# Routing eight chunks as five singles and a group of three, with x added by matmul and the conditional blocks in the middle

## The chip, the core and the metric

The kernel runs on one core of one Trainium2 chip. The core has five engines with instruction streams of their own: TensorE (PE; its weight loads are shown as PEld), VectorE (DVE), ScalarE (ACT), GpSimd (POOL) and SyncE (SP, which here only issues DMAs). They meet through semaphores. Matmuls write to PSUM; everything else lies in SBUF or in DRAM. The metric is the device time of one execution in microseconds.

## What is computed

One transformer block on x of 4096 tokens by 256, in float32: adaptive layer norm, a linear attention, and a mixture of 8 experts of which each token takes 2. Cut to what matters here:

```python
h = _layernorm(x) * (1 + ca) + sa
x = x + ga * attention(h)
h = _layernorm(x) * (1 + cb) + sb
gate_probs = softmax(h @ Wg + bg)                 # 8 experts
_, top_idx = jax.lax.top_k(gate_probs, 2)
expert_mask = one_hot(top_idx, 8).sum(-2)
selected = gate_probs * expert_mask
selected = selected / (selected.sum(-1, keepdims=True) + 1e-08)
y = gelu(h @ W1[e] + b1[e]) @ W2[e] + b2[e]       # for each expert e, H = 1024
x = x + gb * sum_e(selected_e * y_e)
```

## The kernel before

**Layout.** The 4096 tokens are 8 chunks of 512 (`NCH`), each 4 tiles of 128 (`TPC`). `xs[i]` holds chunk i, `hT[i]` its normalized transpose. Attention is folded into one matrix `weff` of 256 columns (`D`) and 8 more (`E`) that give the attention's part of the gate logits; `raw` holds the part that comes from x. `hT[i] @ weff` is the residual of chunk i.

**Order.** `on.pe`, `on.dve`, `on.act`, `on.pool` and `on.sp` keep each engine's instructions in the order in which the Python code makes them, up to the end of the first five blocks. So the code's order is each engine's queue.

**Routing, per Route.** A `Norm` turns the statistics of x into `rstd` and `shift` (`variance` on DVE, `root` as Sqrt on ACT, `finish` on DVE). `distances` makes logits less their greatest, `power` is Exp on ACT, `rows` writes the normalized rows on ACT, `choose` finds the two greatest experts with ranks that break ties, `places` counts on PE, with triangular and all-ones matrices, how many earlier tokens took each expert (`both` is the mask of the two), `weigh` normalizes the weights, `aim` turns places into row numbers of the DRAM table `routed`, and `send` lets POOL scatter the rows by indirect DMA, one for each tile and choice, so 8 per chunk. `seen` carries the counts from one route to the next.

**Routes.** Chunks 0, 1 and 2 are routed singly, then a table (`early_table`) says which 256-row blocks of an expert are full already; chunks 3 and 4 are routed together, and 5, 6 and 7 together inside the first blocks. `park(i)` lets ACT take a chunk's residual out of PSUM into `hT[i]`; `add` lets DVE add it to `xs[i]` and take statistics.

**Blocks.** A block is 256 rows (a pair) or 128 rows (a single) of one expert. Its `load` issues the DMAs of w1, b1, the rows (`xg`), w2 and b2 on SP, with expert and first row read from the table `where`. `prepare` transposes the rows on PE (`ptb`) and scales them on ACT (`xT`); `hidden` is 32 matmul records `ph` with 8 Gelus `gl` on ACT; `project` is 16 records `py` per 128 rows, then two DVE steps `y`; `add_to_out` has POOL gather the last 128 rows of the output, add, and scatter them, while other rows are scattered with an adding DMA. The projection of a block comes after the hidden layer of the next. The first 5 blocks (`EARLY`) hold rows of chunks 0 to 2 only, so they may start while later chunks are still being routed; `steps` says what of the last route goes between which of their parts: key (b, 1) after `hidden` of b and `prepare` of the next, (b, 2) after `project`. `late_table` then places all the rest: 23 pairs, 8 singles always, 4 singles under a condition (`once`), 3 under another (`twice`). `order_of` is the fixed order of the 36 unconditional blocks: 12 pairs, then 8 times two pairs and a single. After them come `once` and `twice`.

Tiles at once: `ps_r` has 3 buffers of two PSUM banks for residuals, `rowpool` 4, w1 3, w2 4, `y` 4.

Of the kernel before, what the change touches and what calls it, by code (L numbers as in the profile page):

```python
# [48 lines left out]
def adaln_block_kernel(  # L49
# [590 lines left out]
    later = table.tile([P, NT, E], FP, tag="later", name="later")  # L640

    def residual(i: int, half: int, cols: int):

        po = ps_r.tile([P, 2, 512], FP, tag="r", name="po")
        for z in range(2):
            t = 2 * half + z
            for kb in range(KB):
                on.pe.matmul(
                    po[:, z, :cols],
                    hT[i][:, kb, t * P : (t + 1) * P],  # L650
                    weff[:, kb, :cols],
                    start=(kb == 0),
                    stop=(kb == KB - 1),
                )
        return po
# [24 lines left out]
    def first_logits():  # L680

        pl = ps_s.tile([P, TPC, E], FP, tag="s", name="pl")
        for t in range(TPC):
            for kb in range(KB):
                on.pe.matmul(
                    pl[:, t, :], hT[0][:, kb, t * P : (t + 1) * P], weff[:, kb, D:],
                    start=(kb == 0), stop=(kb == KB - 1),
                )
        return pl

    def parked(i: int):
        return hT[i].rearrange("p kb (z d) -> p (kb z) d", d=D)

    def keep_logits(i: int, half: int, po):
        n = i * TPC + 2 * half
        on.act.activation(later[:, n : n + 2, :], po[:, :, D : D + E], AF.Identity)

    def park(i: int):

        for half, po in enumerate([residual(i, half, D + E) for half in range(2)]):  # L700
            on.act.activation(
                parked(i)[:, 2 * half : 2 * half + 2, :], po[:, :, :D], AF.Identity
            )
            keep_logits(i, half, po)

    def add_half(i: int, half: int, po):
        two = xs[i][:, 2 * half : 2 * half + 2, :]
        on.dve.tensor_tensor(two, two, po[:, :, :D], ALU.add)

    def chunk_stats(i: int):  # L710
        for t in range(TPC):
            stats(i, t)

    def add(i: int):
        on.dve.tensor_tensor(xs[i], xs[i], parked(i), ALU.add)
        chunk_stats(i)

# [49 lines left out]

    seen = table.tile([P, 1, E], FP, tag="seen", name="seen")
    nc.vector.memset(seen, 0.0)

    class Route:
# [13 lines left out]
        def first_greatest(self, hot, src, name):  # L785

            best = self.per_token(f"{name}_best")
            on.dve.tensor_reduce(best, src, AX.X, ALU.max)
            on.dve.tensor_tensor(hot, src, best.to_broadcast(self.full), ALU.is_equal)
            on.dve.tensor_tensor(hot, hot, rank.to_broadcast(self.full), ALU.mult)  # L790
# [13 lines left out]
        def rows(self, c: int = 0):  # L804

            for t in range(TPC):
                n = self.n0 + c * TPC + t
                on.act.activation(
                    self.row[c][:, t, :D], xs[self.chunks[c]][:, t, :], AF.Identity,
                    bias=shift[:, n : n + 1], scale=rstd[:, n : n + 1],  # L810
                )

        def distances(self, added=None):
# [3 lines left out]
            self.prob = prob = self.per_expert("prob")  # L817
            on.dve.tensor_tensor(
                prob, raw[:, tiles, :], later[:, tiles, :] if added is None else added, ALU.add
            )  # L820
            on.dve.tensor_tensor(
                prob, prob, rstd[:, tiles].unsqueeze(2).to_broadcast(full), ALU.mult
            )
            on.dve.tensor_tensor(prob, prob, gate_c[:, 0].to_broadcast(full), ALU.add)
            top = self.per_token("top")
            on.dve.tensor_reduce(top, prob, AX.X, ALU.max)
            on.dve.tensor_tensor(prob, prob, top.to_broadcast(full), ALU.subtract)

        def power(self):
            on.act.activation(self.prob, self.prob, AF.Exp)  # L830

        def choose(self):

            full, prob = self.full, self.prob
            tot = self.per_token("tot")
            on.dve.tensor_reduce(tot, prob, AX.X, ALU.add)
            on.dve.reciprocal(tot, tot)
            on.dve.tensor_tensor(prob, prob, tot.to_broadcast(full), ALU.mult)
            self.hots = gate.tile([P, 2, GT, E], FP, tag="hots", name="hots")[:, :, : self.nt, :]
            self.first_greatest(self.hots[:, 0], prob, "hot1")  # L840
            rest = self.per_expert("rest")
            on.dve.scalar_tensor_tensor(rest, self.hots[:, 0], -4.0, prob, ALU.mult, ALU.add)
            self.first_greatest(self.hots[:, 1], rest, "hot2")
            self.both = self.per_expert("both")
            on.dve.tensor_tensor(self.both, self.hots[:, 0], self.hots[:, 1], ALU.add)
# [15 lines left out]
        def weigh(self):  # L861
            sel = self.prob
            tot = self.per_token("tot2")
            on.dve.tensor_tensor(sel, self.prob, self.both, ALU.mult)
            on.dve.tensor_reduce(tot, sel, AX.X, ALU.add)
            on.dve.tensor_scalar(tot, tot, 1e-8, None, ALU.add)
            on.dve.reciprocal(tot, tot)
            for c, row in enumerate(self.row):
                tiles = slice(c * TPC, (c + 1) * TPC)
                on.dve.tensor_tensor(  # L870
                    row[:, :, D : D + E], sel[:, tiles, :],
                    tot[:, tiles, :].to_broadcast([P, TPC, E]), ALU.mult,
                )
            self.here = gate.tile([P, E], FP, tag="here", name="here")
            on.dve.tensor_reduce(
                self.here, self.both.rearrange("p t e -> p e t"), AX.X, ALU.add
            )

        def aim(self):
            nt = self.nt  # L880
            place = self.per_expert("place")
            on.dve.tensor_tensor(place, self.pp, region.to_broadcast(self.full), ALU.add)
            on.dve.tensor_tensor(seen[:, 0, :], seen[:, 0, :], self.here, ALU.add)
            of_hot = gate.tile([P, 2, GT, E], FP, tag="of_hot", name="of_hot")[:, :, :nt, :]
            on.dve.tensor_tensor(
                of_hot, self.hots, place.unsqueeze(1).to_broadcast([P, 2, nt, E]), ALU.mult
            )
            dest = gate.tile([P, 2, GT, 1], FP, tag="dest", name="dest")[:, :, :nt, :]
            on.dve.tensor_reduce(dest, of_hot, AX.X, ALU.add)
            self.dest = gate.tile([P, 2, GT], I32, tag="dest_i", name="dest_i")[:, :, :nt]  # L890
            on.dve.tensor_copy(self.dest, dest[:, :, :, 0])

        def send(self, *which):

            for t in [c * TPC + t for c in which for t in range(TPC)]:
                for k in range(2):
# [3 lines left out]
                        self.row[t // TPC][:, t % TPC, :],  # L900
# [4 lines left out]

        def rest(self):
            self.places()
            self.weigh()
            self.aim()
            self.send(*range(len(self.chunks)))  # L910
# [25 lines left out]
    def counts(name):  # L936
        pn = psum_of(f"p{name}", 1, E)[:, 0, :]
        on.pe.matmul(pn, ones, seen[:, 0, :], start=True, stop=True)
        cnt = flat(name)
        on.dve.tensor_copy(cnt, pn)  # L940
# [40 lines left out]
    def early_table():  # L981
        cnt = counts("cnt1")
# [10 lines left out]
    def late_table():  # L993
        cnt = counts("cnt2")
# [20 lines left out]
        lookup(EARLY, NB - EARLY, unit_no[:, EARLY:NB], lo, hi, base, P, 2, "t2")  # L1015
# [6 lines left out]
    accs = [parked(0)[:, z, :] for z in range(2)]  # L1022
# [4 lines left out]
    def load(b: int):  # L1027
        nt = tiles_of(b)
        first = nc.values_load(
            where[0:1, 0, b : b + 1], engines=[ENG.SP], min_val=0, max_val=E * N - nt * P,  # L1030
            skip_runtime_bounds_check_because=IN_RANGE,
        )
        e = nc.values_load(
# [297 lines left out]
```

## Time and profile before

| what | value |
|---|---|
| median of three timed runs | 955.17 us (953.33 to 956.97) |
| the profiled execution | 959.75 us, of which its span 958.0 |
| mean granted TensorE clock in it | 0.951 of full speed |
| indirect sends of routed rows | 64, median 971 ns, from 360.8 to 483.6 us |
| ACT_TABLE_LOAD in 342 to 412 us | 8, mean 1283 ns |
| rows on ACT, 128x256, in 342 to 412 us | 20, mean 585 ns |
| add of x and parked residual on DVE, 128x1024 | mean 1218 ns |

The span runs from the first to the last instruction of the program. "Idle before" is the time in which an engine had nothing to do ahead of an instruction, and the name behind the arrow is what the semaphores say ended it; "remote" and "issue" mean that no instruction in the profile is seen to have ended it. Almost all of this stage is recorded under line 36, that of the helper that keeps the order, so the tile names tell the instructions apart.

### The profile page before, as it was taken

The numbers are of one execution on the slowest core, as the hardware profiler recorded it, in microseconds if no ns is written. First come the engines' busy times: TensorE is split into PE (matmuls) and PEld (weight loads), VectorE is DVE, ScalarE is ACT, GpSimd is POOL, SyncE is SP. The second block draws the span as 40 slices with busy tenths as digits, with TensorE's granted clock in tenths as the row PEclk, the third lists the DMA queues.
The fourth block names the chain that finished last, engine by engine and source line by source line (L and its number), as shares of the span: only waits on it lengthen the run. The fifth ranks groups of instructions, "written<-read, shape, count | busy, mean of one in ns | idle before, by whom it ended". The sixth has DMA issues, their size and how long they took to land.

```text
span 958.0 us, 12819 instructions
## 1 busy us (share of the span) xinstructions
PE 871.0 (91%) x4578; PEld 651.7 (68%) x4578; DVE 384.5 (40%) x943; ACT 347.0 (36%) x638; POOL 361.5 (38%) x311
## 2 busy tenths in 40 slices
PE   7979999999999795698569999999999999999991
PEld 4444444555545574586458888888888888888991
DVE  4454553988888747763511111111111111111210
ACT  4314442344444334435123323333343343343250
POOL 2000000588989506463731332333333332322332
PEclk9979999999999997778869999999999999999996
DMA  9999930132000013496477667668778777777730
GB/s 333 351 344 351 351 100 22 60 116 69 1 1 2 1 45 115 165 347 216 148 231 213 194 195 225 184 200 265 219 221 260 228 225 253 229 227 251 227 119 15
DMA packets 124534, 175.23 MB, mean 183 GB/s; under 512 B 12428, under 2 KB 105266, under 8 KB 124468
## 3 DMA queue, kind: packets, MB, share of 16 engines
q1 hardware_dynamic: 113040, 152.78, 49.1%
q0 software_dynamic: 11424, 21.61, 8.9%
q8 instruction: 37, 0.61, 0.3%
q14 instruction: 29, 0.24, 0.1%
q10 hardware_dynamic: 4, 0.00, 0.0%
HBM read 117.69 MB, written 57.71 MB: 183 GB/s over the span
## 4 chain that ended last, share of the span: by engine, by line
PE 81%; DVE 6%; another core or an unknown queue 4%; POOL 2%; DMA 2%; issue 2%; ACT 2%; POOLq 0%; ACTq 0%; DVEq 0%
PE ph L1089 21%; PE py L1107 21%; PE pk L277 12%; PE pq L277 10%; PE ph L36 3%; PE pctx L539 3%; PE py L36 2%; PE po L36 2%; PE ptb L1060 1%; DMA hT<-out_dram,who 1%; POOL qs L36 1%; PE pa L352 1%; PE pp L36 1%; PE pt L175 1%
## 5 line engine op out<-in xcount | busy, mean ns | idle before, releaser
L1096 ACT ACTIVATE gl<-ph,b_sb 128x256 f32<-128x256 f32 (+1 forms) x280 | 122.2, 437 | 270.7 <-PE ph L1089 263.4
L1107 PE MATMUL py<-w_sb,gl 128*128 128x256 f32 x960 | 212.8, 379 | 0.0
L1089 PE MATMUL ph<-xT,w_sb 128*128 128x256 f32 (+1 forms) x1120 | 207.5, 343 | 0.6 <-ACT xT L1063 0.6
L1089 PEld LDWEIGHTS ph<-xT,w_sb 128*128 128x128 f32 x1120 | 184.5, 191 | 20.4 <-ACT xT L1063 0.8
L1107 PEld LDWEIGHTS py<-w_sb,gl 128*128 128x128 f32 x960 | 179.8, 190 | 23.0
L1115 DVE SCALAR_TENSOR_TENSOR y<-py,gs,gb_bc 128x256 f32<-128x256 f32 x60 | 29.0, 483 | 290.2 <-PE py L1107 287.5
L277 PE MATMUL pq<-wq,hT 128*128 128x512 f32 x256 | 118.3, 604 | 1.2 <-DVE qs L36 1.2
L277 PE MATMUL pk<-wk,hT 128*128 128x512 f32 x256 | 116.2, 606 | 0.3 <-ACT hT L178 0.3
L36 POOL DMA_INDIRECT hT<-out_dram,who x35 | 36.7, 1050 | 141.2 <-DMA out_dram<-hT,who 120.4
L36 POOL DMA_INDIRECT routed<-row,dest_i x64 | 67.3, 1051 | 58.8 <-DVE st L36 19.3
L277 PEld LDWEIGHTS pk<-wk,hT 128*128 128x128 f32 x256 | 48.2, 194 | 60.1 <-issue 55.1
L36 POOL DMA_INDIRECT out_dram<-y,who x33 | 52.4, 1589 | 96.4 <-DVE y L1116 55.7
L277 PEld LDWEIGHTS pq<-wq,hT 128*128 128x128 f32 x256 | 46.0, 189 | 49.5 <-issue 45.9
L36 POOL TENSOR_TENSOR qs<-qs,qsum 128x1024 f32<-128x1024 f32 x30 | 58.0, 1935 | 15.6 <-DVE qsum L36 15.6
L36 DVE TENSOR_TENSOR qs<-qs,pk 128x1024 f32<-128x1024 f32 x31 | 37.8, 1221 | 62.3 <-ACT ka L438 44.1
L36 PE MATMUL ph<-xT,w_sb 128*128 128x256 f32 x160 | 42.4, 421 | 19.7 <-issue 15.8
L36 POOL TENSOR_TENSOR hT<-hT,y 128x256 f32<-128x256 f32 x35 | 25.2, 720 | 81.7 <-DVE y L1116 41.9
L36 PEld LDWEIGHTS ph<-xT,w_sb 128*128 128x128 f32 x160 | 32.9, 211 | 28.0 <-issue 17.4
L36 ACT ACTIVATE qs<-qs 128x1024 f32<-128x1024 f32 x32 | 33.7, 1055 | 38.3 <-DVE qs L36 38.3
L438 ACT ACTIVATE ka<-pk 128x1024 f32<-128x1024 f32 x24 | 24.6, 1024 | 57.6 <-PE pk L277 57.6
L36 DVE TENSOR_REDUCE qmax<-pq 128x16 f32<-128x1024 f32 x32 | 38.6, 1206 | 13.9 <-PE pq L277 13.8
L483 POOL MEMSET qs<- 128x8 f32 x8 | 0.8, 115 | 110.3 <-PE pt L175 79.2
(254 smaller groups left out, 972.6 us busy)
## 6 DMA issues: line engine op xcount, KB each, us to landing
w_sb<-in_L_ffn_W_dram SPq DMA_DIRECT2D x80, 1024.0 KB
routed<-pad SPq DMA_DIRECT2D x32, 1088.0 KB
x<-in_L_attn_x_dram SPq DMA_DIRECT2D x16, 512.0 KB
xg<-routed SPq DMA_DIRECT2D x28, 272.0 KB
b_sb<-b_d SPq DMA_DIRECT2D x40, 128.0 KB
out_dram<-x SPq DMA_DIRECT2D x8, 512.0 KB
xg<-routed SPq DMA_DIRECT2D x12, 136.0 KB
ka<-in_L_wmod_dram SPq DMA_DIRECT2D x3, 512.0 KB
```

The source lines that it names most:

```text
L36: ins = getattr(self.engine, name)(*args, **kwargs)
L175: on.pe.transpose(pt[:, t * P : (t + 1) * P], src[:, t, kb * P : (kb + 1) * P], ident)
L277: nc.tensor.matmul(pw[:, half * 512 : (half + 1) * 512], hT[i][:, kb, t * P : (t + 1) * P], w[:, kb, half * 512 : (half + 1) * 512], start ...
L352: nc.tensor.matmul(pa[32 * kb : 32 * kb + 32, :], gate_w[:, kb, :], plain(i)[:, kb, :], start=True, stop=True,)
L438: nc.scalar.activation(k_tile(n), pk, AF.Identity)
L483: nc.gpsimd.memset(qs[:, :, (h + 1) * HW - 1 : (h + 1) * HW], 1.0)
L539: nc.tensor.matmul(pctx[g][h * DH : (h + 1) * DH, j, :], ek[:, q * P + h * DH : q * P + (h + 1) * DH], qs[:, q, h * HW : (h + 1) * HW], st ...
L1060: on.pe.transpose(pt[:, j * P : (j + 1) * P], xg[:, j, kb * P : (kb + 1) * P], ident)
L1089: on.pe.matmul(ph[:, :rows], w1_sb[:, kb, hb * P : (hb + 1) * P], xT[:, kb, :rows], start=(kb == 0), stop=(kb == KB - 1),)
L1096: on.act.activation(gl[:, hb, :rows], ph[:, :rows], AF.Gelu_apprx_tanh, bias=b1_sb[:, hb : hb + 1])
L1107: on.pe.matmul(py, gl[:, hb, j * P : (j + 1) * P], w2_sb[:, hb, :], start=(hb == 0), stop=(hb == HB - 1),)
L1115: on.dve.scalar_tensor_tensor(y, py, gs[:, j : j + 1], gb_bc, ALU.mult, ALU.mult)
```

## The change

1. **x through PSUM.** For chunks 0 to 2, `residual` adds x (and `raw`) by one more matmul with the identity into the same accumulation, and `keep` copies the sum to `xs`. Statistics of chunk 0 are taken from PSUM. Chunks 3 to 7 are parked in `hT` and added by DVE as before.
2. **A shorter choice.** `choose` works on `far`, the logits less their greatest, so the first choice is where `far` is 0, and no softmax is needed ahead of it. `weigh` forms the weights from the exponents later. `seen` starts with the experts' regions, so `place` goes, and `here` and `seen` come after `dest`.
3. **Routes.** Chunks 0 to 4 singly, 5 to 7 as a group. Products of later chunks stand between `select` and `places`. The early table counts route 2's choice itself, and is made after the sends of chunk 2 are issued. Weights of block 0 are loaded ahead of its rows.
4. **Steps in the first blocks.** `places`, `aim` and sends of chunk 4 go into `hidden` of block 0, after its fifth Gelu (key (0, 0)). The group's rows are made on POOL; its `choose` comes in (0, 1), its 24 sends together in (1, 2), and `late_table` in (2, 2), with the lookup split into pairs and singles.
5. **Order of blocks.** `order_of` has 8 pairs and a single, then seven times two pairs and a single, then 6 pairs. `once` stands after the first 17 of it, `twice` at the end.

The diff, cut to its core:

```diff
 def residual(i, half, cols):
+        whole = i < FIRST
...
-                    stop=(kb == KB - 1),
+                    stop=(kb == KB - 1 and not whole),
+            if whole:
+                on.pe.matmul(po[:, z, :D], ident, xs[i][:, t, :], start=False, stop=(cols == D))
+                if cols > D:
+                    on.pe.matmul(
+                        po[:, z, D:cols], ident, raw[:, i * TPC + t, :], start=False, stop=True
+                    )
...
+    def keep(i: int, half: int, po, more: bool = True):
+        on.act.activation(parked(i)[:, 2 * half : 2 * half + 2, :], po[:, :, :D], AF.Identity)
+        if more:
+            n = i * TPC + 2 * half
+            on.act.activation(logits[:, n : n + 2, :], po[:, :, D : D + E], AF.Identity)
...
+        def rows_on_pool(self, c: int):
             for t in range(TPC):
                 n = self.n0 + c * TPC + t
+                on.pool.tensor_scalar(
+                    self.row[c][:, t, :D], xs[self.chunks[c]][:, t, :],
+                    rstd[:, n : n + 1], shift[:, n : n + 1], ALU.mult, ALU.add,
+                )
...
         def choose(self):
+            on.dve.scalar_tensor_tensor(hots[:, 0], far, 0.0, ranks, ALU.is_equal, ALU.mult)
+            self.first_one(hots[:, 0], "hot1")
             rest = self.per_expert("rest")
+            on.dve.scalar_tensor_tensor(rest, hots[:, 0], -3e38, far, ALU.mult, ALU.add)
+            best = self.per_token("best2")
+            on.dve.tensor_reduce(best, rest, AX.X, ALU.max)
+            on.dve.tensor_tensor(rest, rest, best.to_broadcast(full), ALU.is_equal)
+            on.dve.tensor_tensor(hots[:, 1], rest, ranks, ALU.mult)
+            self.first_one(hots[:, 1], "hot2")
...
+            if hb == HB // 2:
+                for step in steps.get((b, 0), []):
+                    step()
...
-    routes = [Route(0), Route(1), Route(2), Route(3, 4), Route(5, 6, 7)]
+    routes = [*(Route(i) for i in range(NCH - 3)), Route(*range(NCH - 3, NCH))]
...
+    def select(i: int, src=None):
+        r, norm = routes[i], norms[i]
+        norm.variance()
+        norm.root()
+        table_for(AF.Exp)
+        norm.finish()
+        if i >= FIRST:
+            add_logits(i)
+        r.distances(src)
+        r.begin_rows()
+        r.power()
+        r.rows()
+        r.choose()
+    def dispatch(i: int):
+        routes[i].aim()
+        routes[i].send()
+    products(1, 0)
+    select(0, pl)
+    routes[0].places()
+    products(1, 1)
+    park(1)
+    routes[0].weigh()
+    dispatch(0)
...
+    products(3)
+    park(3, 0)
+    select(2)
+    park(3, 1)
+    products(4)
+    routes[2].places()
+    taken_so_far = counts("cnt1", routes[2].both)
+    park(4)
+    routes[2].weigh()
+    dispatch(2)
+    store(2)
+    early_table(taken_so_far)
+    weights = load_weights(0, None)
+    products(5)
+    park(5)
+    products(6)
+    park(6)
     add(3)
+    select(3)
+    products(7, 0)
+    routes[3].places()
+    products(7, 1)
+    park(7)
+    routes[3].weigh()
+    dispatch(3)
     add(4)
+    select(4)
+    routes[4].weigh()
+    table_for(AF.Gelu_apprx_tanh)
+    loads = {0: (load_rows(0), *weights[1:])}
...
     steps = {
-        (0, 1): [lambda i=i: add(i) for i in last.chunks] + [norms[4].iterate, last.distances],
-        (1, 1): [last.power, last.begin_rows, lambda: last.rows(0), lambda: last.rows(1), last.choose],
-        (1, 2): [last.places, last.weigh, last.aim, lambda: last.send(0, 1)],
-        (2, 1): [lambda: last.rows(2), lambda: last.send(2), late_table],
-        (2, 2): [lambda: store(3), lambda: store(4)],
+        (0, 0): [routes[4].places, lambda: dispatch(4)],
+        (0, 1): [
+            *(lambda i=i: add(i) for i in last.chunks),
+            norms[5].iterate,
+            lambda: add_logits(*last.chunks),
+            last.distances,
+            last.begin_rows,
+            *(lambda c=c: last.rows_on_pool(c) for c in range(3)),
+            last.choose,
+        ],
+        (1, 1): [last.power, lambda: table_for(AF.Gelu_apprx_tanh)],
+        (1, 2): [last.places, last.weigh, last.aim, *(lambda c=c: last.send(c) for c in range(3))],
+        (2, 2): [late_table, lambda: store(3), lambda: store(4)],
         (3, 2): [lambda: store(5), lambda: store(6), lambda: store(7)],
     }
-    order_of = list(range(EARLY + PAIRED - 2 * FIXED))
+    pairs, order_of = list(range(EARLY + PAIRED)), []
     for j in range(FIXED):
-        order_of += [EARLY + PAIRED - 2 * (FIXED - j) + z for z in range(2)]
-        order_of.append(EARLY + PAIRED + j)
+        order_of += pairs[: (EARLY + 3 if j == 0 else 2)] + [EARLY + PAIRED + j]
+        del pairs[: (EARLY + 3 if j == 0 else 2)]
+    order_of += pairs
...
-    run(order_of[EARLY:], once[:1])
+    middle = EARLY + 12
+    run(order_of[EARLY:middle], once[:1])
     flush()
     with tc.If(n_left > UNITS):
         run(once, [])
         flush()
+    run(order_of[middle:], [])
+    flush()
     with tc.If(n_left > UNITS + ONCE):
         run(twice, [])
         flush()
```

## The prediction

> **What bounds it now.** All sums are against the profiled execution, 959.75 us with a span of 958.0. The median of the timed runs (955.17) is 4.6 us lower; I work out a difference in us and take it from the median. From the page I read engine shares and slices first:
>
> ```profile
> PE 871.0 (91%) x4578; PEld 651.7 (68%) x4578; DVE 384.5 (40%) x943; ACT 347.0 (36%) x638; POOL 361.5 (38%) x311
> ...
> PE   7979999999999795698569999999999999999991
> ```
>
> PE is full except in slices 15 to 21 and the last. So I cut the span there with the table of windows (length, then each engine's busy us and count, PE clock, DMA share, GB/s):
>
> ```profile
> 342.00:412.30 70.30, 47.54 (x209) 39.59 (x207) 46.58 (x210) 31.26 (x70) 26.27 (x28) 0.82 0.39 138
> 412.30:447.70 35.40, 30.80 (x131) 25.64 (x132) 20.18 (x77) 17.60 (x33) 18.49 (x20) 0.84 0.77 260
> 447.70:515.50 67.80, 48.99 (x209) 40.40 (x208) 19.56 (x68) 15.72 (x34) 34.91 (x31) 0.82 0.65 207
> 515.50:907.90 392.40, 392.40 (x1995) 349.13 (x1994) 66.27 (x199) 137.07 (x310) 125.05 (x116) 1.00 0.74 224
> 907.90:937.80 29.90, 29.24 (x199) 26.97 (x198) 5.32 (x20) 13.73 (x38) 8.54 (x10) 1.00 0.37 123
> 937.80:958.00 20.20, 0.00 (x0) 0.00 (x0) 0.97 (x2) 0.00 (x0) 5.44 (x6) 0.62 0.05 15
> ```
>
> The rows: routing until ph of block 0 starts; blocks 0 and 1; blocks 2 to 4; the other 31 fixed blocks, in which PE never stops; the four conditional blocks (40 pairs of weight loads on the page, so `once` runs and `twice` doesn't); a tail without PE. The change adds no block, so row four can hardly move. What can move is 173.5 us in the first three rows, where PE works 127, and the 20.2 us tail.
>
> The timelines by engine tell what holds them. First routing, then the worst hole, with POOL beside it:
>
> ```profile
> 400.67 0.20 DVE L36 RECIPROCAL rstd<-rstd 128x8 f32<-128x8 f32 x1 [3.71 <-ACT rstd L36]
> 406.43 0.69 PE L36 MATMUL pp<-both,before 128*128 128x64 f32 x2 [8.14 <-DVE both L36]
> ```
> ```profile
> 456.07 2.07 ACT L36 ACTIVATE row<-x,shift,rstd 128x256 f32<-128x256 f32 x4
> 482.77 0.47 ACT L36 ACTIVATE gl<-ph,b_sb 128x256 f32<-128x256 f32 x1 [24.64 <-remote]
> 483.30 2.07 PE L36 MATMUL ph<-xT,w_sb 128*128 128x256 f32 x4 [14.33 <-issue]
> 470.18 0.97 POOL L36 DMA_INDIRECT routed<-row,dest_i  x1 [0.30 <-issue]
> ```
>
> In routing PE waits for DVE's chain to `both`. In the hole no compute holds anybody: PE had done ph's first groups by 466, yet ACT is let go at 482.8, while POOL issues a send every 1.27 us. I call it the **crawl**. It shows three times, each inside a run of sends: sends from 360.8, DVE gaps from 378.9 to 383.8; from 412.6, ACT late from 425.7 to 436.5; from 451.1, ACT and PE late from 465.6 to 489.9. So it starts 13 to 18 us into unbroken sends and ends 2 to 5 us after them; the eight sends from 386.1 (12 us) show none. Why, the trace doesn't tell; I use it as a rule of this trace.
>
> **Part 1: shorter routes, x in PSUM.** Small DVE steps follow each other every 0.22 us. `choose` falls from 15 to 10, `distances` from 5 to 4 for chunks 0 to 2, and `here`, `seen` and `place` leave the way to `dest`: some 8 steps, 1.8 us of a route that takes 11.1 us (359.8 to 370.9). The add of x (1.29 us per chunk) leaves DVE. PE gets eight more identity records per chunk at 0.216 us, 1.7 us, plus some 0.4 for the logits: hidden, as PE waits 5.0 and 6.7 us for `both` there; without that cover it costs three times 2.1. ACT keeps 128x512 halves at 0.60 as before. `choose` no longer waits for Exp. Stepping the new order through with these rows, `both` of routes 0, 1, 2 comes at 354.2, 364.5, 373.7 (was 357.6, 367.5, 381.2). Sends 0 and 1 (8 x 1.27 = 10.2 each) now run from 357.5 to 378 unbroken, so I keep the 3.4 us that the crawl costs DVE: `dest` of route 2 at 379.7, `where` at 384.9 (was 390.0).
>
> **Part 2: chunks 3 and 4 singly.** Before, one double route: 396.8 to 411.6. Now two, on DVE: add 3.4 until 388.4; but `root` waits on ACT for the parks of chunks 5 and 6 (PE 4.4 per chunk as in 385 to 398, done near 391) and a 1.28 table load, to 392.3; 3.7 to `both` (396), pp 1.6 and aim 1.0 (398.6), add of chunk 4 3.4 (402), norm and choose 4 (406). ACT's rows end near 406.2, the Gelu table 407.5, xT 1.0, ph of block 0 at 408.7. **-3.6 us.** That is little, since the serial route gives back most of part 1. [...] The row here is 1283 ns a load, with the next activation 0.02 us behind it (399.13 to 400.43). [...] Should each route still cost its old 11 us, ph starts near 422.
>
> **Part 3: the first blocks.** `places` and `aim` of route 4 go into ph of block 0 (pp 1.9 us on PE); its 8 sends run near 417 to 427, alone, so the crawl of 425 to 436 should not come. The group's chain on DVE: three adds 10.3 from 417, iterate 3.3, distances 1.5, choose 2.8, `both` near 435, as py of block 0 ends. It no longer waits for ACT (13.25 us idle before `tot` at 440.25). Ph of block 2 then starts 30.1 us after ph of block 0 (9.5 cold, pp 1.9, xT 1.2, ph 7.1, transposes and py 7.4, pp 3.0), against 35.4. **-5.3 us.** The twelve rows go from ACT (0.5 each) to POOL, unseen there: nearest row POOL TENSOR_TENSOR 128x256, 720 ns, which reads two inputs; so 8.6 us at most, nearer 7; 432 to 439.5. It is behind sends 4 and ahead of the last sends, so each us lost beyond `aim` at 440 delays those. From below nothing, as `aim` hides it.
>
> **Part 4: the last 24 sends.** Unbroken, 24 x 1.27 = 30.6, from 440 to 471, then two scatters of 1.6. Crawl from 453.5 to 476 or so; before, the run lasted 37.2 us with its scatters, from 3.4 us after ph of block 2, now some 35.5 from 1.2 after. Ph of block 3 lies in it as before and ends near 477; py, ph, py (7.4 each) follow, block 5 at 500. From ph of block 2 that is 61.2 against 67.8. **-6.6 us.** `late_table` now starts as the crawl does (before it ran 455.4 to 467.7, ahead of it); its some 60 steps may be held to the end, where near 480, block 5's rows at 485 for a transpose at 492. Cover 7 us; what exceeds it is paid. SP: the row load of block 5 queues behind its w1 and b1, and behind it w2, b2 and the stores of chunks 3 and 4; all of those are later needed.
>
> **Part 5: `once` in the middle.** Its loads are issued by SP ahead of PE: before, SP reached the end of the body at 919.5 and PE at 937.7, so the blocks behind it are fetched in time. New is a transpose with no other work on PE before block order_of[17] and one ph without py behind it: 1.3 + 0.7. **+2.0 us.** [...] The view of L1294 has branches of 38 to 180 ns, and ACT's next instruction 0.16 us later. [...]
>
> The tail: PE is done at 937.7, but POOL is two blocks behind, as single blocks need a gather, add and scatter of 6.5 us in sequence:
>
> ```profile
> 937.71 1.05 POOL L36 DMA_INDIRECT hT<-out_dram,who  x1 [2.22 <-DMA out_dram<-hT,who]
> 937.83 0.48 DVE L1115 SCALAR_TENSOR_TENSOR y<-py,gs,gb_bc 128x256 f32<-128x256 f32 x1 [2.52 <-PEq L1297]
> 948.03 1.00 POOL L36 DMA_INDIRECT out_dram<-hT,who  x1 [0.28 <-POOL hT L36]
> ```
>
> With pairs last (14.25 us of PE each, POOL's chain about 12) the backlog is gone: the last gather lands about 1.5 us after PE's end, add 1.0, scatter 1.0, landing 2.4, then the closing 7.5 (950.5 to 958) stays: 14 for 20.2. **-6.3 us.**
>
> **Sum.** -3.6 -5.3 -6.6 +2.0 -6.3 = -19.8: span 938.2, execution 940.0, median **935**.
>
> **Rivals.** (a) The crawl's long hole goes too, as the rows and the send of chunk 7 no longer sit between scatters: 20 us of PE back, 915. For it: eight sends show none; against: 24 unbroken are the longest run yet. (b) Single routes cost their old 11 us: ph of block 0 at 422 instead of 408.7, 949. [...] (d) **Slower:** POOL gets dest so early that sends 0 to 4 run unbroken from 357 to past 410, and DVE and ACT crawl through routes 2, 3 and 4: in the first crawl 13 DVE steps lost 3.4 us, 0.26 each. These routes have about 110 steps, 29 us; less the 3.4 in my sum that is +25: 961. It decides from some 75 slowed steps on. For it: sends 0 and 1 already join. Against: a crawl delays the next dest, which breaks the run and ends it, and 4 us of pause before 386.1 sufficed.
>
> **Chances.** Forecast 0.50, its own range 924 to 947 (both ends of the rows above: rows on POOL, Sqrt drains, table in the crawl). (a) 0.13, (b) 0.15, (c) 0.06, (d) 0.16. About 0.5%, 4.8 us, can be told from no change. Faster: all of the forecast, (a) and (c), and just over half of (b): 0.78; same 0.07, from (b); slower 0.15. Range 916 to 955: it leaves out (d) and the edge of (a).
>
> **What would show it.** Ph of block 0 near 409, of block 2 near 439, L1089's successor near 500; no late ACT between sends 4 and the last group; a hole of 20 to 25 us in ph of block 3; no PE idle over 2 us after the body of `once`; 14 us from PE's last matmul to the end. I am wrong if the crawl lies in routes 2 to 4, if row four grows by more than 3 us, or if the table holds block 5.

## The result, and the profile after

The changed kernel takes **959.40 us** (median of 20 runs, 951.51 to 963.16) where the kernel before takes 954.04 beside it (20 runs): ratio 1.0053, 95% interval 1.0030 to 1.0075. It is slower by half a per cent; 935 was predicted. The profiled execution of after took 959.42 us and lies at its median, that of before (959.75) 5.7 above its own, so the two spans, 957.7 and 958.0, show no difference, and the stages are to be read one by one.

The page of the changed kernel, engine shares and PE's slices:

```profile
PE 880.1 (92%) x4636; PEld 660.8 (69%) x4636; DVE 380.2 (40%) x950; ACT 347.7 (36%) x637; POOL 366.4 (38%) x323
...
PE   7979999999999798569759999999999999999993
```

Slices 16 to 21 hold as little of PE as before; only the last slice has visibly gained. The table of windows, cut at the same events as before (ph of blocks 0, 2 and 5, the last 30 us of PE, PE's end):

```profile
342.00:418.27 76.27, 55.98 (x257) 47.22 (x258) 41.85 (x207) 38.07 (x81) 32.04 (x36) 0.82 0.49 176
418.27:451.47 33.20, 30.77 (x140) 26.61 (x141) 22.16 (x81) 12.86 (x25) 19.14 (x26) 0.86 0.50 177
451.47:518.26 66.79, 48.77 (x207) 41.23 (x207) 18.80 (x74) 14.09 (x30) 33.10 (x31) 0.82 0.54 176
518.26:913.20 394.94, 392.39 (x2053) 350.15 (x2052) 66.00 (x212) 145.00 (x335) 125.99 (x119) 1.00 0.75 234
913.20:943.30 30.10, 30.04 (x142) 26.10 (x140) 4.84 (x10) 6.12 (x13) 8.79 (x8) 1.00 0.14 28
943.30:957.70 14.40, 0.00 (x0) 0.00 (x0) 0.97 (x2) 0.00 (x0) 4.53 (x4) 0.62 0.14 27
```

Row 1 ends 6.0 us later than before (412.3), row 2 is 2.2 shorter, row 3 1.0 shorter, rows 4 and 5 together 2.7 longer, the tail 5.8 shorter. The back of the program did what was forecast. Its front, which was to give 15.5 us, lost 2.8. The timelines say where, routing first:

```profile
369.13 0.22 DVE L36 TENSOR_TENSOR of_hot<-hots,pp 128x64 f32<-128x64 f32 x1 [3.14 <-PE po L36]
393.62 0.60 ACT L36 ACTIVATE hT<-po 128x512 f32<-128x512 f32 x1 [15.66 <-remote]
394.34 6.89 PE L36 MATMUL po<-weff,hT 128*128 128x264 f32 x16 [6.99 <-ACT logits L36]
400.49 0.18 DVE L36 RECIPROCAL rstd<-rstd 128x4 f32<-128x4 f32 x1 [4.59 <-ACT rstd L36]
418.27 2.07 PE L36 MATMUL ph<-xT,w_sb 128*128 128x256 f32 x4 [6.67 <-ACT spare L36]
...
483.02 0.97 POOL L36 DMA_INDIRECT routed<-row,dest_i  x1 [0.30 <-issue]
489.84 0.47 ACT L36 ACTIVATE gl<-ph,b_sb 128x256 f32<-128x256 f32 x1 [27.93 <-remote]
490.18 1.22 PE L36 MATMUL ph<-xT,w_sb 128*128 128x256 f32 x2 [14.92 <-DVE cnt L36]
```

The crawl has come back in both runs of sends. In routing, sends 1 and 2 are unbroken from 370.7 to 391.0, and ACT, which has to park chunk 5, is let go at 393.62, and PE, which waits for the same PSUM buffers, at 394.34. The rest of the parks, Sqrt and the second half of `norm` (400.49) come behind, and ph of block 0 is nearly 10 us later than the forecast of 408.7. In block 3, ACT stands 27.93 us and PE 14.92 beside the last 24 sends.

### The profile page after: what moved, and what is told of

Same layout as the page of the kernel before. It is cut to its first block, busy times and chain, and to the rows that moved or that the text cites. A ratio compares the mean times of both kernels' runs of the same rounds, so it can differ in the third digit from the quotient of the medians.

```text
span 957.7 us, 12945 instructions
## 1 busy us (share of the span) xinstructions
PE 880.1 (92%) x4636; PEld 660.8 (69%) x4636; DVE 380.2 (40%) x950; ACT 347.7 (36%) x637; POOL 366.4 (38%) x323
## 5 line engine op out<-in xcount | busy, mean ns | idle before, releaser
L1129 PEld LDWEIGHTS ph<-xT,w_sb 128*128 128x128 f32 x1120 | 184.4, 191 | 22.1 <-ACT xT L1103 2.7
L36 POOL DMA_INDIRECT routed<-row,dest_i x64 | 65.1, 1017 | 65.1 <-DVE st L36 18.4
L36 PE MATMUL ph<-xT,w_sb 128*128 128x256 f32 x160 | 44.8, 441 | 25.3 <-DVE cnt L36 14.9
L36 PEld LDWEIGHTS ph<-xT,w_sb 128*128 128x128 f32 x160 | 35.5, 226 | 33.1 <-DVE cnt L36 15.8
L36 ACT ACTIVATE qs<-qs 128x1024 f32<-128x1024 f32 x32 | 33.8, 1055 | 38.2 <-DVE qs L36 38.2
L36 PE MATMUL po<-weff,hT 128*128 128x264 f32 (+1 forms) x128 | 38.8, 455 | 7.0 <-ACT logits L36 7.0
L36 DVE TENSOR_REDUCE qmax<-pq 128x16 f32<-128x1024 f32 x32 | 38.6, 1206 | 13.9 <-PE pq L277 13.8
```

The lines of the kernel that those rows point to most:

```text
L36: ins = getattr(self.engine, name)(*args, **kwargs)
L1129: on.pe.matmul(ph[:, :rows], w1_sb[:, kb, hb * P : (hb + 1) * P], xT[:, kb, :rows], start=(kb == 0), stop=(kb == KB - 1),)
```

## Experiments

Theory **T**: on this chip a run of unbroken sends holds the other engines up, and a break of a few us without a send starts the count anew. Rival **U**: the stretch is set by the serial routes, the parks and the table loads, and the holes are only their waiting. Theory **C**, added after the first four runs: the crawl belongs to the occasion (the chip, or the time) and not to the kernel alone, and the changed kernel loses more to it than the kernel before. Runs sent together ran on one chip, with the kernel before beside them. That matters here, and the column "crawl" says whether the trace of the run has an ACT hole of 10 us or more that "remote" ended, ahead of block 5.

| run | edit | us | before beside it | ratio (95%) | crawl |
|---|---|---|---|---|---|
| result | changed kernel | 959.40 | 954.04 | 1.0053 (1.0030 to 1.0075) | twice |
| e1_pause_early | + pause ahead of sends 1, 2 | 926.83 | 934.64 | 0.9910 (0.9883 to 0.9937) | none |
| e2_pause_late | + pauses in the last 24 | 940.52 | 934.64 | 1.0048 (1.0032 to 1.0064) | none |
| e3_middle_alone | before + part 5 | 930.69 | 934.64 | 0.9948 (0.9927 to 0.9969) | none |
| e5_pause_both | + both pauses | 937.89 | 934.64 | 1.0024 (1.0009 to 1.0039) | none |
| c1_after_again | changed kernel | 958.60 | 954.00 | 1.0042 (1.0019 to 1.0066) | twice |
| c2_before_again | kernel before | 958.96 | 954.00 | (one run) | once |
| c3_pause_early_again | as e1 | 951.77 | 954.00 | 0.9989 (0.9970 to 1.0008) | late only |
| c4_pause_late_again | as e2 | 948.77 | 954.00 | 0.9941 (0.9922 to 0.9960) | early only |
| f1_five_five | shorter pauses, both | 935.73 | 953.90 | 0.9809 (0.9777 to 0.9841) | none |
| f2_rows_between | rows as pauses | 935.45 | 953.90 | 0.9799 (0.9761 to 0.9837) | none |
| f3_twelve_twelve | one late pause | 938.81 | 953.90 | 0.9829 (0.9798 to 0.9861) | late only |
| f4_once_last | part 5 undone | 961.92 | 953.90 | 1.0067 (1.0032 to 1.0103) | twice |
| h1_before_breaks | before + breaks | 941.03 | 934.93 | 1.0052 (1.0036 to 1.0068) | none |
| h2_before_breaks_middle | the same + part 5 | 935.63 | 934.93 | 1.0010 (0.9990 to 1.0031) | none |
| h3_after_beside | changed kernel | 925.96 | 934.93 | 0.9895 (0.9862 to 0.9928) | none |
| h4_rows_between_again | as f2 | 933.26 | 934.93 | 0.9967 (0.9951 to 0.9982) | none |
| k1_before_breaks_again | as h1 | 940.33 | 936.48 | 1.0058 (1.0033 to 1.0082) | none |
| k2_before_breaks_middle_again | as h2 | 937.10 | 936.48 | 1.0014 (0.9999 to 1.0029) | none |

### First four: pauses, and the middle alone

```diff
+        def pause(self, n: int):
+            for _ in range(n):
+                on.pool.memset(idle, 0.0)
...
         routes[i].aim()
+        if 0 < i < FIRST:
+            routes[i].pause(8)          # e1, e5
         routes[i].send()
...
-        (1, 2): [..., *(lambda c=c: last.send(c) for c in range(3))],
+        (1, 2): [..., send(0), pause(8), send(1), pause(8), send(2)],   # e2, e5
```

For e1_pause_early:

> The changed kernel with 8 memsets of an unused 128x512 tile put on POOL ahead of the sends of chunk 1 and ahead of those of chunk 2, an estimated 4 to 5 us without a send each time. Theory T (a run of unbroken sends is what holds PE, ACT and SP up; a break of 4 us or more starts the count anew): the hole of ACT at 378 to 394 us (15.66 us, released by 'remote') falls below 5 us, the logits and parks of chunks 5 and 6 end some 8 us sooner, products of block 0 start at 408 to 412 instead of 418.3, and the time is some 8 us below the changed kernel's, about 951 us. Rival U (the serial routes, the parks on ACT and the two table loads set this stretch, and the hole is their waiting): the pauses only push the sends back, products of block 0 start at 418 to 422, 959 to 963 us.

For e2_pause_late:

> The changed kernel with the same pause of 8 memsets after the first and after the second eight of the last group's 24 sends. Theory T: the hole of ACT that ended at 489.8 us (27.93 us) falls below 10 us and PE's of 14.92 us below 5, although the last scatter ends some 9 us later; block 5's products start no later than in the changed kernel, at best 10 to 15 us sooner; 945 to 959 us. Rival U (the engines wait for the count of block 3 and 4's rows or for one another): holes stay at 25 us or more or grow by the pauses, 959 to 968 us.

For e5_pause_both:

> The changed kernel with both sets of pauses. Theory T: the two gains add, 940 to 951 us, below the kernel before. Rival U: the delays add, 960 to 972 us.

For e3_middle_alone, the kernel before with the changed kernel's `order_of`, and `once` after its first 17 blocks:

> The kernel before with only the new order of blocks and the conditional blocks in the middle (12 blocks after the early ones); routing, parks and the last group as before. By the trace of the changed kernel the middle costs +2.8 us between the first later block and PE's end and saves 5.7 in the tail: 3 us below the kernel before, ratio 0.997 (0.994 to 0.999). If the rest of the changed kernel shifts this (its lead over the loads at that point differs), the ratio is 1.000 or above.

These could not test T: on this chip there was nothing to cure. The kernel before took 934.64 us instead of 954, and no trace has a "remote" hole, not even e2's, whose sends of chunks 0 to 2 run unbroken from 357.1 to 388.9. The late pauses then cost their length and more (e5 less e1: 11 us; the two took 4.6 and 4.7 in c4), as the rows of block 5 wait for the last scatter (PE 9.35 us for them in e2). Part 5 alone is worth 0.5%, 4.9 us by the ratio, against 4.3 in the prediction's sum (+2.0 and -6.3).

### The same again, beside both kernels

Nothing is edited here but as in e1 and e2. For c1_after_again and c2_before_again, the two kernels as they are:

> The changed kernel once more. In the four runs so far no engine was let go late by 'remote' (in one of them the last 24 sends are unbroken as in the changed kernel), and the kernel before took 934.6 us where it took 954.0 beside the changed kernel. Theory C (the crawl belongs to the occasion, not to the kernel: it comes and goes between runs of the same program, and the changed kernel loses to it more than the kernel before): if the kernel before is again at 934 to 936 us, the changed kernel has no 'remote' hole, its products of block 0 start near 405, and it takes 924 to 929 us, ratio 0.988 to 0.994; if the kernel before is near 954, the holes are there and the ratio is 1.003 to 1.008. Theory T (unbroken sends alone bring it): the hole of 15 us at 378 to 394 is there in any case, ratio 1.003 or above.

> The kernel before once more, for its trace. Theory C: at a time near 934 us, PE's hole of 14.33 us ahead of block 4's second tile and ACT's of 24.63 us are gone, and from the products of block 2 to those of the first later block it is some 15 us less than the 67.8 us of the first trace. Theory T: the hole is there, as the kernel is the same.

For c3_pause_early_again and c4_pause_late_again:

> The early pauses (8 memsets on POOL ahead of the sends of chunks 1 and 2) beside the changed kernel itself. If there is no crawl in the changed kernel: within 3 us of it, 0 to 3 us slower, since the pauses only push sends back. If there is one: theory T says that it goes, 8 us below the changed kernel; rival U that it stays, 0 to 4 us above.

> The late pauses (after the first and second eight of the last 24 sends) beside the changed kernel itself. If there is no crawl: block 5's rows wait for the last scatter, which ends some 10 us later, and it takes 10 to 13 us more than the changed kernel. If there is one: theory T, ACT's hole of 27.93 us falls below 10 and it takes up to 10 us less than the changed kernel; rival U, the holes stay and it takes 0 to 9 us more.

This chip shows the crawl in both kernels, and here T can be tested. Timeline of c3 (pauses early): the break, the park of chunk 5, and a Gelu of block 3:

```profile
380.52 4.61 POOL L36 MEMSET idle<- 128x512 f32 x8
383.22 0.60 ACT L36 ACTIVATE hT<-po 128x512 f32<-128x512 f32 x1 [7.24 <-PE po L36]
481.02 0.47 ACT L36 ACTIVATE gl<-ph,b_sb 128x256 f32<-128x256 f32 x1 [28.04 <-remote]
```

Timeline of c4 (pauses late): the same park, a pause, a Gelu of block 3, and PE's one longer wait there:

```profile
393.51 0.60 ACT L36 ACTIVATE hT<-po 128x512 f32<-128x512 f32 x1 [15.66 <-remote]
463.34 4.62 POOL L36 MEMSET idle<- 128x512 f32 x8
468.72 0.47 ACT L36 ACTIVATE gl<-ph,b_sb 128x256 f32<-128x256 f32 x1 [7.05 <-PE ph L36]
498.30 1.08 PE L36 MATMUL ptb<-ident,xg 128*128 128x128 f32 x4 [9.32 <-DMA xg<-routed]
```

Each pause removes the hole in its own place and leaves the other: 15.66 "remote" against 7.24 behind PE, and 28.04 "remote" against 7.05 behind PE. Products of block 0 start at 409.57 in c3 (419.79 in c1). The late pauses bring a new wait, 9.32 us for the rows of block 5, and still leave the kernel 9.8 us faster than c1; the early ones leave it 6.8 faster. U had each of them level or slower. **T holds on this chip, but not everywhere: in the first four runs 24 unbroken sends held nobody. So C holds as well.** Each set of runs had one chip, and only the chip of e1 to e5 was used again (h1 to h4), both times without the crawl; whether it goes with the chip or with the occasion is not shown. In c2 the kernel before crawls too, but less (ACT 18.73, PE 9.85 us).

### How long a break, how long a run

```diff
+        if i == 2:
+            routes[i].pause(5)          # f1; 3 in f2, 8 in f3
...
-            *(lambda c=c: last.rows_on_pool(c) for c in range(3)),
+            lambda: last.rows_on_pool(0),                               # f2
...
-        (1, 2): [..., *(lambda c=c: last.send(c) for c in range(3))],
+        (1, 2): [..., send(0), pause(5), send(1), pause(5), send(2)],   # f1
+        (1, 2): [..., send(0), rows_on_pool(1), send(1), rows_on_pool(2), send(2)],   # f2
+        (1, 2): [..., send(0), send(1, 0, 2), pause(8), send(1, 2, 2), send(2)],      # f3
```

For f1_five_five and f2_rows_between:

> The changed kernel with 5 memsets (some 3.1 us) ahead of the sends of chunk 2 only, and 5 after the first and second eight of the last group. Where the crawl shows (kernel before near 954): theory T' (3 us without a send are enough to start the count anew; the natural break of 3.1 us ahead of chunk 1's sends was): both holes gone, products of block 0 near 408, no 'remote' hole in block 3, and the gains of the early and the late pauses add: 7 + 10 and some 4 us less spent on pausing, 936 to 944 us, ratio 0.982 to 0.990. If 3 us are too few (rival), holes of 10 us or more stay in both places, ratio 1.00 or above. Where no crawl shows (before near 935): 929 to 935 us, late pauses costing some 6 us.

> The changed kernel with 3 memsets (some 1.9 us) ahead of the sends of chunk 2, and the rows of the last group's chunks 6 and 7 made on POOL between its sends (2.2 us each, work that is moved and not added). Where the crawl shows: if 2 us are enough, both holes go and it is 2 to 4 us faster than with pauses of 3 us, 934 to 941 us; if 2 us are too few, as the break of 2.2 us in the kernel before's sends suggests (its hole ended 2 to 10 us after that break), holes of 10 us or more stay, 950 to 960 us. Where no crawl shows: 926 to 932 us.

For f3_twelve_twelve:

> The changed kernel with 8 memsets (some 5 us) ahead of the sends of chunk 2, and one such pause in the middle of the last 24 sends (twelve and twelve, 15.3 us each). Where the crawl shows: if it needs a run of more than 15 us, no hole; 938 to 945 us. If it starts at 13 us (lower end seen), short holes of 2 to 6 us at the end of each twelve; 942 to 950 us. Where no crawl shows: 929 to 934 us.

For f4_once_last, the changed kernel with the old order of blocks and all conditional blocks last:

> The changed kernel with the kernel before's order of blocks, the conditional ones last (part 5 undone). By the traces it costs the tail 5.7 us and saves 2.8 in the body: 3 to 4 us slower than the changed kernel, 962 us and ratio 1.008 (1.005 to 1.011) where the crawl shows. Where none shows: routing and first blocks alone are worth what the early-pause kernel had (0.991) less the middle's 0.005, ratio 0.993 to 0.997. If part 5 were what makes the change slow, the ratio is at or below 1.000 where the crawl shows.

On this chip, which crawls, the changed kernel with breaks in both places is 18 us below the kernel before. The windows of f2, cut as before (from 342 us to ph of block 0, then to ph of blocks 2 and 5), and from its timeline a break and the wait that is left:

```profile
342.00:408.66 66.66, 51.99 (x257) 44.94 (x256) 41.94 (x204) 37.92 (x81) 33.33 (x38) 0.86 0.46 159
408.66:439.09 30.43, 28.73 (x141) 24.77 (x141) 20.30 (x76) 12.85 (x25) 13.72 (x18) 0.92 0.75 270
439.09:493.07 53.98, 46.19 (x208) 40.05 (x207) 20.68 (x79) 14.31 (x30) 34.56 (x36) 0.91 0.60 193
```
```profile
452.22 2.15 POOL L36 TENSOR_SCALAR row<-x,rstd,shift 128x256 f32<-128x256 f32 x4
482.71 1.08 PE L36 MATMUL ptb<-ident,xg 128*128 128x128 f32 x4 [7.79 <-DMA xg<-routed]
```

In f2, breaks of 2.1 to 2.7 us between eights (end of one send to start of the next) were enough against the long holes. There the late ones add no work to POOL, which has to make these rows anyway, but the last 24 sends then take 35.1 us (442.2 to 477.4) instead of 30.5, and the rows of block 5 are waited for. f1 and f2 are the versions that beat both kernels where the crawl shows. A run of 12 sends was too long in one of two places of f3 (ACT held 14.98 us). Timeline of f3, end of the first twelve, then of the second:

```profile
467.86 1.57 ACT L36 ACTIVATE gl<-ph,b_sb 128x256 f32<-128x256 f32 x4 [8.95 <-PE ph L36]
484.61 0.97 POOL L36 DMA_INDIRECT routed<-row,dest_i  x1 [0.30 <-issue]
488.99 1.20 ACT L36 ACTIVATE gl<-ph,b_sb 128x256 f32<-128x256 f32 x3 [14.98 <-remote]
489.52 2.07 PE L36 MATMUL ph<-xT,w_sb 128*128 128x256 f32 x4 [5.27 <-ACT gl L36]
```

The second twelve started at 470.44; PE stops at 484.25, 14 us later, and is let go 3.9 us after the last send. At the first twelve (15.1 us) ACT is only some 2 us late: the first Gelu of block 3 starts 3.05 us after its ph (464.81), where c4 has 1.15. The expectation had a hole at both or at neither. f4 is not better than the changed kernel (1.0067 against 1.0053 and 1.0042, with intervals that overlap), so part 5 is not what makes the change slow.

### What the change is worth without the crawl, and the kernel before with breaks

```diff
             for t in [c * TPC + t for c in which for t in range(TPC)]:
+                if t % TPC == 0 and self.chunks[0] + t // TPC in (1, 4, 6, 7):
+                    for _ in range(5):
+                        on.pool.memset(idle, 0.0)
```

The edit is to the kernel before, for h1 and k1; h2 and k2 add part 5. For h1_before_breaks and h2_before_breaks_middle:

> The kernel before with 5 memsets (some 3.1 us) on POOL ahead of the sends of chunks 1, 4, 6 and 7, so that no more than eight sends follow each other. Where the crawl shows: if the crawl was most of what the kernel before loses too (PE idle 14 us in block 3, table and parks late), 934 to 942 us, ratio 0.980 to 0.988, and the breaks, not the change, are what wins. If the change's own steps carry the gain: 948 to 952 us, ratio 0.994 to 0.998.

> The same, and part 5 alone of the change (order of blocks, conditional ones in the middle): 3 to 5 us below the former, whatever that is. What the changed kernel with breaks is faster than this is worth parts 1 to 4.

For h3_after_beside and h4_rows_between_again:

> The changed kernel beside the others. Where the crawl shows: ratio 1.003 to 1.008. Where none shows: ratio 0.988 to 0.994.

> The changed kernel with breaks of some 2 us (rows of chunks 6 and 7 between the sends, 3 memsets ahead of chunk 2's), beside the kernel before with breaks. Where the crawl shows: ratio 0.977 to 0.983 as it had. If parts 1 to 4 are worth what was predicted of routing and first blocks without the crawl (3.6 + 5.3 us), it is 5 to 9 us below the kernel before with breaks and the middle; if within 2 us of it, parts 1 to 4 bring nothing and only breaks and middle count.

For k1_before_breaks_again and k2_before_breaks_middle_again:

> The kernel before with breaks, once more, for a chip that shows the crawl (kernel before near 954). There: if the breaks and not the change are what wins, ratio 0.980 to 0.988; with 6 us for the breaks themselves, as the chip without the crawl had it, and a crawl that costs the kernel before 19 us (954 less 935), 941 us and 0.986. If the crawl stays in it, ratio 1.000 to 1.006. On a chip that shows none: 1.005 again.

> The same with part 5, for a chip that shows the crawl: 5 us below the former, 936 us, ratio 0.981, which would be level with the changed kernel with breaks (0.980), so that parts 1 to 4 are worth 2 us or less there. If parts 1 to 4 are worth their 5 to 9 us, ratio 0.986 to 0.990. On a chip that shows none: 1.001 again.

Neither chip crawled. So the changed kernel without the crawl is on record, h3, first its windows, then its timeline at the places shown of the crawling one:

```profile
342.00:407.92 65.92, 52.32 (x258) 44.76 (x256) 41.98 (x204) 37.94 (x81) 33.00 (x35) 0.86 0.50 170
407.92:441.10 33.18, 30.76 (x141) 26.67 (x141) 22.30 (x81) 12.87 (x25) 19.28 (x26) 0.86 0.68 244
441.10:486.28 45.18, 44.87 (x207) 39.02 (x207) 18.62 (x73) 14.23 (x30) 28.26 (x27) 0.96 0.63 204
```
```profile
365.93 0.22 DVE L36 TENSOR_TENSOR of_hot<-hots,pp 128x64 f32<-128x64 f32 x1 [0.30 <-PE pp L36]
378.12 0.99 POOL L36 DMA_INDIRECT routed<-row,dest_i  x1 [0.28 <-POOL row L36]
383.80 0.60 ACT L36 ACTIVATE hT<-po 128x512 f32<-128x512 f32 x1 [7.23 <-PE po L36]
```

The same program, now 1.05% faster than the kernel before. All 24 early sends run unbroken (357.2 to 389.0), as rival (d) feared, and nobody is held up. From ph of block 2 to ph of block 5 PE has 44.87 busy us in 45.18, where it had 48.77 in 66.79. Rows 1 and 3 alone differ between the two traces of this kernel, by 10.35 and 21.6 us, which is all but 1 us of the 33.0 between the spans. Without the crawl, parts 1 to 4 are worth some 5 us (0.9895 for the whole change against 0.9948 for part 5 alone); with breaks in both kernels only 2.4 are left (h4 against h2), fewer than the 5 to 9 of the expectation.

Breaks are no gift where nothing crawls: they cost the kernel before 0.5% (h1, k1) and the changed one 7 us (h4 less h3), as breaks delay the last scatter and with it the rows of block 5. In h1 PE waits 11.94 us for them (5.08 in e3, the kernel before with part 5 and without breaks), in h4 4.33 (0.32 in h3):

```profile
490.11 1.09 PE L36 MATMUL ptb<-ident,xg 128*128 128x128 f32 x4 [11.94 <-DMA xg<-routed]
```

What the kernel before would gain from breaks on a chip that crawls was asked twice, and both times the runs fell on a chip that does not; it **stays open**. The edit would not have parted all sends either: in h1 the break ahead of chunk 1 pushes its sends up to those of chunk 2, and 16 run unbroken (379.1 to 401.3). The lead of f2 there (0.980) can't be divided between the breaks and the change.

## Why the prediction was wrong

The steps, in us, as the prediction's own terms (ph of block 0; from there to block 2; from there to block 5; to PE's end; tail):

| step | before | predicted | after | after, no crawl (h3) | with breaks, crawling chip (f2) |
|---|---|---|---|---|---|
| ph of block 0 | 412.3 | 408.7 | 418.3 | 407.9 | 408.7 |
| to block 2 | 35.4 | 30.1 | 33.2 | 33.2 | 30.4 |
| to block 5 | 67.8 | 61.2 | 66.8 | 45.2 | 54.0 |
| to PE's end | 422.2 | 424.2 | 425.0 | 424.4 | 424.9 |
| tail | 20.2 | 13.9 | 14.4 | 14.0 | 13.6 |

Of the 19.5 us by which the span of 957.7 exceeds the forecast of 938.2, 9.6 arise ahead of ph of block 0, 3.1 up to block 2, 5.6 up to block 5 and 1.3 behind it. The rest of the miss in the median comes of the trace of before, which lay above the median from which the sum was taken.

**Part 1 failed**, in one term: "I keep the 3.4 us that the crawl costs DVE". The steps themselves were right: `both` of routes 0 and 1 came at 354.26 and 364.62 (forecast 354.2 and 364.5), and without the crawl or with breaks, ph of block 0 comes at 407.9 to 408.7. But the crawl was carried over as what it had cost in its old place, where 13 small DVE steps stood beside it. The trace of before shows ACT held there too, at a park (first line), and the prediction put that at nothing. In its new place stood the parks of chunks 5 and 6 on ACT, with PE's buffers behind them: 15.66 us for ACT. The parks were to be done near 391; the table load that follows them starts at 398.96 (second line, after) and without the crawl at 388.62 (third line, h3):

```profile
381.65 0.60 ACT L36 ACTIVATE hT<-po 128x512 f32<-128x512 f32 x1 [3.19 <-remote]
398.96 1.28 ACT L36 ACT_TABLE_LOAD   x1
388.62 1.28 ACT L36 ACT_TABLE_LOAD   x1
```

That is 8 of the 9.6 us by which ph of block 0 is late. The crawl also began earlier than the 13 us of my rule: PE was done with the places of route 1 at 366.3, 8.7 us after the first send, and DVE read them 3 us late (369.13, against 365.93 without the crawl). So eight sends were enough for a hold of 3 us. All eight traces of the changed kernel and its variants on crawling chips have it, with 3.0 to 3.2 us of idle time ahead of that step, f1 and f2 too; the five on the other chip have 0.3. It parted sends 0 from sends 1, which the prediction had joined, and sends 1 and 2 ran together instead.

**Part 2**: the two serial routes and their table loads cost 1.6 us more than reckoned: 19.3 from the end of the parks to ph of block 0, in after (398.9 to 418.3) and in h3 (388.6 to 407.9), against 17.7 (391 to 408.7). The row of 1283 ns held: the load at 398.96 took 1.28 us and the next activation began 0.01 behind it. No run shows the "Sqrt drains" that the prediction's range allows for. Rival (b) is out: without the crawl ph of block 0 comes at 407.9 (h3), not near 422.

**Part 3**: the crawl beside sends 4 did go, as forecast. Of the 3.1 us over the forecast 2.9 are PE's clock, not a wait. PE idles 2.43 us in this row in the changed kernel and in f4 alike, but at a granted clock of 0.86 and 0.95, and its busy times, 30.77 and 27.86 us, are in the ratio of these clocks; the window of f4 in which the row takes 30.29:

```profile
416.90:447.19 30.29, 27.86 (x141) 24.14 (x141) 21.06 (x75) 12.85 (x25) 17.66 (x26) 0.95 0.52 184
```

Why the clock differs there no run settles. The rows on POOL took 0.54 us each in the break shown of f2 (2.15 for four), under the 0.72 taken as their upper end.

**Part 4 failed** in the place of ph of block 3: its end was put near 477, 38.2 us after ph of block 2, and it came 45.4 after. The run of sends, with the scatter right behind it, was sized well (32.5 us from 453.5), but ph was thought to be done when they end. It had 16 of its 32 records left and took 6.6 us more, because PE does not go slowly in the crawl's late part but stands (14.92 us). `late_table`, for which 7 us of cover were kept, did not hold anybody up by its length: PE was let go by its first step, `cnt`, but DVE itself had been held until 489.05, and from 490.2 PE runs through to block 5. The 67.8 us from which the gain was taken were one sample, too: in c2, the other trace of the kernel before, this row took 63.6 (451.62 to 515.22).

**Part 5** held: +2.7 to PE's end against +2.0, no wait over 1.23 us on PE around the middle branch (whose body runs in these traces, so that a jump over it is not tested), and a tail 5.8 us shorter against 6.3. No run shows a stall at that branch, which chance (c) is for: in rows 4 and 5 of the windows PE is busy for 422.43 of 425.04 us. In the timeline of after, the last gather now comes at PE's end and the last scatter 4.1 us behind it:

```profile
944.09 1.18 POOL L36 DMA_INDIRECT hT<-out_dram,who  x1 [4.53 <-DMA out_dram<-hT,who]
948.23 1.03 POOL L36 DMA_INDIRECT out_dram<-hT,who  x1 [0.28 <-POOLq L1380]
```

Rival (d) had the time (961) and the kind of cause, more unbroken sends early, but not its mechanism: not 75 DVE steps late by 0.26 each, but one hold of ACT; routes 3 and 4 were free of it. That 961 is near 959.4 is chance: (d) put 25 us into the routes, where 9.6 were lost. Its counter-argument, that a crawl delays the next `dest` and so breaks the run, is what parted sends 0 and 1.

Behind these terms is one choice. The prediction took the crawl for a property of the kernel, "a rule of this trace", and sized three gains by it. It depends on the chip or the occasion as much as on the kernel. By the medians, and if the chips differ in nothing else, the crawl costs the kernel before 19 us (954.0 less 934.9) and the changed kernel 33 (958.6 less 926.0). The change itself gains 9; the crawl takes 13.6 more from it than from the kernel before; 4.6 us slower is what remains. Why sends bring it stays open.

## What to carry to other kernels

When the profile shows idle time that no instruction ends ("remote", "issue" on several engines at once), treat its length as unknown wherever the work around it moves: price the move once with the hole absent and once with it on the engine that now stands beside it. Break long runs of indirect sends with POOL work that has to be done anyway, at most eight sends to a run here, but only where the stall is: such breaks (f2, h4) made the changed kernel 23 us faster on chips with it and 7 slower on one without. Measure a change of half a per cent on more than one chip, since this one was 0.5% slower on some and 1% faster on another.

## What the hardware showed that was not expected

Whether the crawl shows goes with another mark. The list of DMA issues has, as its last column, the median time to landing, given only where no record of a DMA's landing is missing. Changed kernel on the crawling chip, then the same kernel as h3:

```profile
routed<-row,dest_i POOLq DMA_INDIRECT x64
```
```profile
routed<-row,dest_i POOLq DMA_INDIRECT x64, 2.8
```

In every trace from the crawling chips the list has a landing for none of the 440 DMAs; in every trace from the others, for 436 or more. Counted in the traces, 5,568 to 6,021 records of landings stand against 7,015 to 7,027. Up to 355 us all traces have the same (1,027 to 1,043); from 355 to 525 us, where the sends run, those from crawling chips have 858 to 1,242 and the others 2,004 to 2,128. f1 and f2, without a hole of 10 us, lack almost as many as the rest. So on the crawling chips records are missing and engines are let go late in the same stretch. "Remote" may then say no more than that the record of the release is missing, but a hole's length rests on start times, and the medians show it.

No run here shows why the records are missing or why the engines are let go late, and none tells whether an execution that is not recorded would crawl; the cause is not settled. What is shown is that on these chips eight sends brought a hold of 3 us (3.14 in the trace of after) and some longer runs brought holes of 15 us and more (14.98 at the second twelve of f3, the shortest run with one), that breaks of 2.1 to 2.7 us kept such holes away (f2), and that on other chips 24 unbroken sends held nobody up (e2, h3).
